# One core, 32 images of 32 channels: the sum r formed later, modes reordered earlier, a fuller end phase

## The chip, the cores and the metric

The kernel runs on one core of one Trainium2 chip. The metric is the device time of one execution in microseconds; the time before is the median of three executions.

## The reference

The input x has 32 images of 32 channels of 128 x 128 numbers, all in float32. Two layers are computed, each as x plus an operation on the group-normalised x (16 groups of 2 channels).

```python
# layer 0: a matrix square root of each channel by five Newton-Schulz steps
normA = jnp.sqrt(jnp.sum(A2 * A2, axis=(1, 2)))
Y = A2 / normA[:, None, None]; Z = I
for _ in range(5):
    T = 0.5 * (3.0 * I - jnp.matmul(Z, Y))
    Y = jnp.matmul(Y, T); Z = jnp.matmul(T, Z)
x = x + (Y * jnp.sqrt(normA)[:, None, None])
# layer 1: a spectral convolution; only 64 x 32 modes are kept
x_dht = jnp.fft.fftn(gn(x), axes=(2, 3)).real
top = jnp.einsum('bixy,ioxy->boxy', x_dht[:, :, :32, :32], weights1)
bot = jnp.einsum('bixy,ioxy->boxy', x_dht[:, :, -32:, :32], weights2)
x = x + jnp.fft.ifftn(out_dht, axes=(2, 3)).real   # out_dht holds top and bot, zeros elsewhere
```

## The kernel before

**Unit of work.** Layer 0 works on groups of four channels, 256 in all, each a tile of 128 x 512. `newton` (line 423) is a generator that carries one group: two calls of `quartic` (line 387), a few products between them, and a last sum into `xt`. A matrix product of a group is four matmuls of 128 x 128 (`products`, line 327), which in the profile are eight MATMUL records. `quartic` forms v from a product, turns it, adds `r` to make `w`, and multiplies v and w. `r` is the input plus a multiple of the identity: `plus_eye` (line 313), one GpSimd (POOL) instruction.

**Near and far groups.** For images 1 to 18 (`is_far`, line 339) the transpose of v goes partly through memory: VectorE (DVE) transposes blocks into `turn`, SyncE (SP) writes it to DRAM and reads it back as `w` (lines 394 to 409), and POOL adds r (line 411). For the other images TensorE (PE) transposes v, and DVE adds r from PSUM in the same instruction (line 415).

**Order of the work.** Nothing is left to a scheduler: the class `Engine` (line 75) keeps every engine's instructions in the order in which the program issues them. The main loop (line 1027) runs in rounds. In each round nine lanes take one step of their generator each; `yield from rest` (line 421) is two yields, so the next part of a group is issued two rounds later. A new group starts every three rounds (far) or five (near). Between lanes the loop steps other queues of generators: `norms` (scaling of the next group's input, `staged`, line 356), `posts` and `specs` (the forward transform of finished images, `forward` and `spectrum`), `prods` in two of three rounds (the products of modes with weights), and `backs` in one of three rounds, and when a batch is held (the inverse transform, `inverse`, line 863). When no lane is left, `tail` is true (line 1028) and all queues are stepped in every slot; the output stores then go out on ScalarE's (ACT's) queue instead of SP's (line 848).

**Where r stands before.** The first r of a group is issued at the end of `staged` (line 384), before the group starts, and waits there for ACT's scaling of `b`. The second is issued right after ACT's copy of `mb` (line 435). POOL takes its work in order, and other lanes' sums w stand behind these.

**Modes.** Images are taken in four sets of 20, 7, 3 and 2 (`GROUPS`). After the last image of a set its modes are multiplied: `wide_products` (line 603), `small_products` (line 659, sets of 7 and 3) and `last_products` (line 736, the last two images). The results go to DRAM (`od`) and come back per image: `load_products` (line 809) loads `or`; for the small sets a copy puts the modes in order as `ob` (line 872), 1.94 us on ACT in the median; then `inverse` issues 8 matmuls with `ob`, copies the result as `gt`, and runs two batches (e = 0, 1) of 8 matmuls, sums `yt` with DVE, unfolds them with POOL or DVE, and stores them. `load_input` (line 828) reads back the image into `yt` buffers, of which there are six, and three shared with `fold` at the end. `weights` (line 778) loads the last set's weights into tiles that the last lanes no longer need.

Of the kernel before, what the change touches and what calls it, by code (L numbers as in the profile page):

```python
# [36 lines left out]
P = 128  # L37
# [16 lines left out]
NB = 8  # L54
# [34 lines left out]
def conv_preact_kernel(  # L89
# [77 lines left out]

    def bank():
        return ps8.tile([P, 4, P], F32, tag="ps", name="ps")

    def root(v, n, tag):

# [183 lines left out]
    def staged(b, g, nm, sc, off, sn):  # L356

        m = four("x", has_more(b, g))
        xt, mb = raw.pop((b, g))

        def on_scalar(t, x, offset, scale, c):
            c = slice(c, c + 1)
            kept(
                nc.scalar.activation(t, x, AF.Identity, bias=offset[:, c], scale=scale[:, c])
            )

        for j in range(4):
            c = 4 * g + j
            if j < 2 or not is_far(b):
                kept(  # L370
                    nc.gpsimd.tensor_scalar(
                        m[:, j, :],
                        xt[:, j, :],
                        nm[:, c // 2 : c // 2 + 1],
                        sc[:, c : c + 1],
                        ALU.add,
                        ALU.mult,
                    )
                )
            else:  # L380
                on_scalar(m[:, j, :], xt[:, j, :], off, sc, c)
            on_scalar(mb[:, j, :], mb[:, j, :], off, sc, c)
            yield
        ready.append((xt, m, mb, plus_eye(mb, is_far(b), has_more(b, g))))
        yield

    def quartic(m, mb, r, far, more, wide):


        v = plus(m, -QA * MS, products(mb, m), "v", more)  # L390
        if far:


            t = four("turn", more)
            form = "p c (b i) -> p b c i" if wide else "p c (i b) -> p b c i"
            nc.vector.transpose(blocks(t), v.rearrange(form, b=4))
            held = dram.tile([P, 512], F32, name="turn", tag="turn", bufs=8)
            kept(nc.sync.dma_start(out=held, in_=t.rearrange("p c x -> p (c x)")))
            yield from rest
            w = four("w", more)  # L400
            wb = blocks(w).rearrange("p a c j -> p a (c j)")
            if wide:
                for b in range(4):
                    rows = slice(32 * b, 32 * b + 32)
                    src = held[:, P * b : P * b + P].rearrange("(a i) x -> i a x", a=4)
                    kept(nc.sync.dma_start(out=wb[rows], in_=src))
            else:
                src = held.rearrange("(a i) (b x) -> (i b) a x", a=4, b=4)
                kept(nc.sync.dma_start(out=wb, in_=src))
            yield from rest  # L410
            nc.gpsimd.tensor_tensor(w, w, r, ALU.add)
            w = blocks(w).rearrange("p a c j -> p c a j")
        else:
            yield from rest
            w = plus(transposed(v), 1.0, r, "w", more)
        yield from rest
        q = plus(products(v, w), QF / (16 * MS**4), eye, "q", more)
        yield from rest
        return q

    rest = (None, None)

    def newton(g, sn, xt, m, mb, r, far, more):


        q = yield from quartic(m, mb, r, far, more, False)
        my = four("my", more)
        y = my[:, :, 0, :]
        nc.scalar.mul(y, products(q, m), 1 / (MS * QF))
        yield from rest  # L430
        m = my[:, :, 1, :]
        nc.scalar.mul(m, products(q, y), MS / QF)
        yield from rest
        mb = taken(transposed(m), "mb", more)
        r = plus_eye(mb, far, more)
        yield from rest
        q = yield from quartic(m, mb, r, far, more, True)
        both = [bank().rearrange("p (j k) x -> p j k x", k=2) for _ in range(2)]
        for j in range(4):
            nc.tensor.matmul(both[j // 2][:, j % 2], q[:, j], my[:, j], start=True, stop=True)  # L440
        w, y = four("t", more), four("y4", more)
        for h in range(2):
            nc.scalar.mul(w[:, 2 * h : 2 * h + 2, :], both[h][:, :, 1, :], 1 / (MS * QF))
        for j in range(4):
            c = 4 * g + j
            nc.scalar.mul(y[:, j, :], both[j // 2][:, j % 2, 0, :], sn[:, c : c + 1])
        yield from rest
        t = plus(products(w, q), -0.5 * EYE / (1.5 * QF), eye, "t", more)
        yield from rest
        nc.vector.tensor_tensor(xt, products(t, y), xt, ALU.add)  # L450
        yield

    folds = {}
# [88 lines left out]
    def spectrum(b, u):  # L542
# [40 lines left out]
        if i == len(xs):  # L583

            for e, t in enumerate(diags):
                for l4 in range(4):
                    rows = slice(32 * l4, 32 * l4 + 32)
                    copy = nc.scalar.copy if l4 % 2 else nc.vector.tensor_copy
                    copy(
                        t.rearrange("p (m b l f) -> p m b l f", b=2, l=4, f=4)[rows, :, j, l4, :],  # L590
                        spec[rows, 8 * e : 8 * e + 8].rearrange("p k q (h f) -> p (k q h) f", f=4),
                    )
            yield
            return
        kept(
# [63 lines left out]
    def small_products(i):  # L659
# [40 lines left out]
        done = None  # L700
        for kk in range(KK):
            yield
            k2, e = divmod(kk, 2)
            wt, xk = wts[kk % len(wts)], xks[k2 % len(xks)]
            if not e:
                pm = bank()
            for t in range(8):
                for q in range(4):
                    nc.tensor.matmul(
                        pm[32 * q : 32 * q + 4 * n, 2 * e + t // 4, 32 * (t % 4) : 32 * (t % 4) + 32],  # L710
                        xk[:, :, 32 * e + 8 * q + t],
                        wt[:, t // 4, q, t % 4, :],
                        start=True,
                        stop=True,
                    )
            if kk + len(wts) < KK:
                load_weights(kk + len(wts))
            if done and not e:
                store(*done)
            if e:  # L720
                om = page(f"om{i}_{k2}")[:, 0:512]
                for j, rows in enumerate(parts):
                    copy = nc.vector.tensor_copy if j % 2 else nc.scalar.copy
                    copy(om[rows], pm.rearrange("p a x -> p (a x)")[rows])
                done = k2, om
                if k2 + len(xks) < KK // 2:
                    load_spectra(k2 + len(xks))
# [8 lines left out]
    def last_products(i):  # L736
# [4 lines left out]
        for kk in range(KK):  # L741
# [25 lines left out]
            if kk % 4 == 3:  # L767
                for f in range(4):
                    queue = nc.scalar if f % 2 else nc.sync
                    kept(  # L770
                        queue.dma_start(
                            out=od[i][f, kk - 3 : kk + 1].rearrange("k r x -> r k x"),
                            in_=om[f::4, :, f, :].rearrange("p (k h) o -> p k (h o)", h=2),
                        )
                    )
        yield

    def weights():
# [74 lines left out]
    def unfold():  # L853

        while sums:
# [4 lines left out]
                engine.tensor_tensor(yh, yh, d, op)  # L860
            stores.append((b, o, y))

    def inverse(b):


        more = where[b][1] < GROUPS[where[b][0]] - 1
        load_products(b)
        load_input(b, 0)
        yield
        ob = obs[b]  # L870
        if GROUPS[where[b][0]] <= NB:
            ob = inv.tile([P, 1024], F32, tag="ob", name=f"ob{b}", bufs=2)
            if where[b][0] == len(GROUPS) - 1:
                for h, copy in enumerate((nc.scalar.copy, nc.vector.tensor_copy)):
                    copy(
                        ob.rearrange("p (o h f l) -> p h o f l", h=2, f=4, l=4)[:, h],
                        obs[b].rearrange("p (f l h o) -> p h o f l", f=4, l=4, h=2)[:, h],
                    )
            else:
                nc.scalar.copy(  # L880
                    ob.rearrange("p (o t l) -> p o t l", t=8, l=4),
                    obs[b].rearrange("p (l t o) -> p o t l", l=4, t=8),
                )
        ob = ob.rearrange("p (e j m) -> p e j m", e=2, j=4)
        if more:
            load_products(b + 1)

# [8 lines left out]
        for e in range(2):  # L896
            gts.append(inv.tile([P, 4, P], F32, tag="gt", name=f"gt{b}_{e}", bufs=3))
            nc.scalar.copy(gts[e], pg[e])
        unfold()
        yield  # L900
        for e in range(2):
# [33 lines left out]
                load_input(b, 1)  # L935
            elif more:
                load_input(b + 1, 0)
            yield
        if not more:
            unfold()  # L940
# [194 lines left out]
```

## Time and profile before

| | |
|---|---|
| median of three executions | 3071.15 us (3064.79, 3072.52, 3071.15) |
| profiled execution | 3066.71 us |
| its span, first to last instruction | 3064.9 us |
| mean granted TensorE clock | 0.981 |
| PE, DVE, ACT, POOL busy | 95%, 73%, 54%, 65% |
| POOL sums r<-mb and r<-b | 256 each, mean 1275 ns |
| DMA | 636.41 MB, mean 208 GB/s |

In the profile's lines all recorded operations have line L83, since a helper issues them; so groups are told apart by the names of their tiles: `ps<-w,v` is a matmul into PSUM from w and v. A wait reads "engine tile <- engine tile that released it: us in total, times, longest". In a timeline a row is: start, duration, engine, line, operation, tiles, count, and in brackets the idle time before it with what ended it. PEld is TensorE's loading of weights, SPq and ACTq are issues of DMAs.

### The profile page before, as it was taken

What the parts mean: (1) busy time and instruction counts of PE and PEld (TensorE: products, weight loads), DVE (VectorE), ACT (ScalarE), POOL (GpSimd) and SP (SyncE); (2) the same over time, 40 slices, a digit from 0 to 9 for tenths busy, and PEclk for the clock granted to TensorE, in tenths of its full rate; (3) what the DMA queues carried; (4) which work ended last, traced back from release to release, by engine and by line L of the source; (5) the groups of instructions that cost most, each with busy time, mean ns of one, the idle gap of its engine ahead of it and who ended that gap; (6) DMA issues with size and microseconds to landing.
All of it is one profiled execution on the core that took longest, in us unless ns stands there. A gap on an engine that the chain in (4) does not pass through costs nothing. (4 is left out here: it accounts for less than half of the span.)

```text
span 3064.9 us, 73467 instructions
## 1 busy us (share of the span) xinstructions
PE 2897.2 (95%) x27076; PEld 2689.8 (88%) x27076; DVE 2244.1 (73%) x4255; ACT 1644.0 (54%) x4187; POOL 1997.2 (65%) x2312
## 2 busy tenths in 40 slices
PE   6999999999999999999999999999999998899984
PEld 6899999999989999989999888889889988888873
DVE  6778787868787788778876655777778766666564
ACT  3565555555656565656544445555555554554552
POOL 3667676767767677767764434778777764667453
PEclk9999999999999999999999999999999999999996
DMA  5476666667676767676742467767768677664675
GB/s 170 157 230 200 209 211 205 214 194 225 189 234 191 231 194 231 193 214 208 233 139 90 151 200 232 244 227 249 259 204 275 231 258 218 203 200 158 198 241 196
DMA packets 476660, 636.41 MB, mean 208 GB/s; under 512 B 97040, under 2 KB 257296, under 8 KB 476304
## 3 DMA queue, kind: packets, MB, share of 16 engines
q1 hardware_dynamic: 362976, 424.31, 43.2%
q10 hardware_dynamic: 113328, 207.41, 21.7%
q8 instruction: 217, 3.56, 0.5%
q14 instruction: 139, 1.14, 0.1%
HBM read 402.42 MB, written 229.11 MB: 206 GB/s over the span
## 5 line engine op out<-in xcount | busy, mean ns | idle before, releaser
L83 PE MATMUL ps<-my,q 128*128 128x128 f32 (+1 forms) x4096 | 734.5, 329 | 3.2 <-DVE w L83 1.5
L83 PEld LDWEIGHTS ps<-my,q 128*128 128x128 f32 x4096 | 625.6, 191 | 61.1 <-issue 6.8
L83 POOL TENSOR_TENSOR r<-mb,eye 128x512 f32<-128x512 f32 x256 | 326.5, 1275 | 431.6 <-ACT mb L83 413.3
L83 PE MATMUL ps<-w,v 128*128 128x128 f32 x4096 | 557.0, 279 | 34.3 <-POOL w L83 26.0
L83 PEld LDWEIGHTS ps<-w,v 128*128 128x128 f32 x4096 | 504.9, 193 | 53.9 <-POOL w L83 34.9
L83 ACT ACTIVATE b<-b,a_off,a_sc 128x128 f32<-128x128 f32 x1024 | 469.6, 493 | 150.9 <-issue 45.8
L83 DVE SCALAR_TENSOR_TENSOR q<-ps,eye 128x512 f32<-128x512 f32 x512 | 350.9, 685 | 225.5 <-PE ps L83 219.8
L83 ACT ACTIVATE my<-ps 128x512 f32<-128x512 f32 x512 | 306.4, 603 | 377.9 <-PE ps L83 361.7
L83 POOL TENSOR_TENSOR r<-b,eye 128x512 f32<-128x512 f32 x256 | 326.4, 1275 | 214.7 <-ACT b L83 160.4
L83 POOL TENSOR_TENSOR fold<-xt 128x256 f32<-128x256 f32 x512 | 363.6, 732 | 128.5 <-DVE xt L83 126.6
L83 POOL TENSOR_TENSOR w<-w,r 128x512 f32<-128x512 f32 x288 | 365.1, 1275 | 121.0 <-DMA w<-turn 94.8
L83 POOL TENSOR_TENSOR yt<-yt,d 128x512 f32<-128x512 f32 x248 | 310.8, 1279 | 147.7 <-ACT d L83 110.4
L83 ACT ACTIVATE t<-ps 128x256 f32<-128x256 f32 x512 | 191.4, 381 | 373.4 <-PE ps L83 361.5
L83 POOL TENSOR_SCALAR x<-xt,a_nm,a_sc 128x128 f32<-128x128 f32 x736 | 322.6, 451 | 18.6 <-DVE a_n L83 18.6
L83 ACT ACTIVATE y<-ps,a_t_s 128x128 f32<-128x128 f32 x1024 | 290.4, 374 | 0.0
L83 PE MATMUL ps<-y,t 128*128 128x128 f32 x2048 | 276.9, 279 | 8.1 <-DVE t L83 5.8
L83 PE MATMUL ps<-x,b 128*128 128x128 f32 x2048 | 277.3, 279 | 5.7 <-POOL x L83 5.7
L83 PE MATMUL ps<-x,q 128*128 128x128 f32 x2048 | 275.7, 278 | 3.2 <-DVE q L83 3.2
L83 PE MATMUL ps<-my,mb 128*128 128x128 f32 x2048 | 276.9, 279 | 0.0
L83 PE MATMUL ps<-q,t 128*128 128x128 f32 x2048 | 274.8, 277 | 0.5 <-DVE u L83 0.5
L83 DVE STREAM_TRANSPOSE turn<-v 128x512 f32<-128x512 f32 x288 | 264.8, 919 | 9.9
L83 PEld LDWEIGHTS ps<-y,t 128*128 128x128 f32 x2048 | 254.8, 194 | 13.0 <-issue 6.6
(121 smaller groups left out, 4464.7 us busy)
## 6 DMA issues: line engine op xcount, KB each, us to landing
turn<-turn SPq DMA_DIRECT2D x288, 256.0 KB
b<-in_x ACTq DMA_DIRECT2D x256, 256.0 KB
xt<-in_xt ACTq DMA_DIRECT2D x256, 256.0 KB
xs<-in_xs ACTq DMA_DIRECT2D x256, 256.0 KB
mid<-xt SPq DMA_DIRECT2D x256, 256.0 KB
yt<-mid SPq DMA_DIRECT2D x128, 512.0 KB
out<-yt SPq DMA_DIRECT2D x117, 512.0 KB
w<-turn SPq DMA_DIRECT2D x144, 256.0 KB
```

What stands on the lines that cost most here:

```text
L83: return self.tc.keep_in_program_order(issue(*args, **kw))
```

## The change

`plus_eye` is no longer called in `staged` and in `newton`; `quartic` calls it itself, two rounds after v for far groups (where the reload of `w` is issued) and one round after v for near groups, in place of one of its two plain yields. A new function `place` holds the copy that puts modes in order; `inverse` calls it for the next image of its set at the end of its last batch, with a step of its own for the first image of a set. In the end phase `inverse` loads both images' modes at its start and places the second image's modes right after the copies of `gt`. `small_products` yields twice at odd `kk`. A new function `warm` issues matmuls of 128 x 512 whose result nothing reads: two after the last group's `newton`, two after the last image's spectrum, nine after `last_products`.

```diff
+    def warm(n):
+        ps = bank()
+        for _ in range(n):
+            nc.tensor.matmul(ps, ident, tab[:, 0:512], start=True, stop=True)
...
-        ready.append((xt, m, mb, plus_eye(mb, is_far(b), has_more(b, g))))
+        ready.append((xt, m, mb))
...
             kept(nc.sync.dma_start(out=held, in_=t.rearrange("p c x -> p (c x)")))
             yield from rest
+            r = plus_eye(mb, far, more)
             w = four("w", more)
...
         else:
-            yield from rest
+            yield
+            r = plus_eye(mb, far, more)
+            yield
             w = plus(transposed(v), 1.0, r, "w", more)
...
         mb = taken(transposed(m), "mb", more)
-        r = plus_eye(mb, far, more)
         yield from rest
...
         nc.vector.tensor_tensor(xt, products(t, y), xt, ALU.add)
+        if not todo and lanes.count(None) == LANES - 1:
+            warm(2)
...
+            if tail:
+                warm(2)
             yield
             return
...
         for kk in range(KK):
             yield
+            if kk % 2:
+                yield
...
+        warm(9)
         yield
...
+    placed = {}
+
+    def place(b):
+        if GROUPS[where[b][0]] > NB:
+            placed[b] = obs[b]
+            return
+        ob = placed[b] = inv.tile([P, 1024], F32, tag="ob", name=f"ob{b}", bufs=2)
...
     def inverse(b):
...
         load_products(b)
+        if tail and more:
+            load_products(b + 1)
         load_input(b, 0)
         yield
-        ob = obs[b]
...
+        if b not in placed:
+            place(b)
+            if not tail:
+                yield
+        ob = placed.pop(b).rearrange("p (e j m) -> p e j m", e=2, j=4)
         if more:
             load_products(b + 1)
...
             nc.scalar.copy(gts[e], pg[e])
+        if tail and more:
+            place(b + 1)
         unfold()
         yield
...
             elif more:
                 load_input(b + 1, 0)
+                if b + 1 not in placed:
+                    place(b + 1)
             yield
```

More of the change, by code (lines that the diff above doesn't have):

```diff
@@ L383, in staged, with quartic @@
             yield
-        ready.append((xt, m, mb, plus_eye(mb, is_far(b), has_more(b, g))))
+        ready.append((xt, m, mb))
         yield
-    def quartic(m, mb, r, far, more, wide):
+    def quartic(m, mb, far, more, wide):
         v = plus(m, -QA * MS, products(mb, m), "v", more)
@@ L421, in conv_preact_kernel, with newton @@
     rest = (None, None)
-    def newton(g, sn, xt, m, mb, r, far, more):
-        q = yield from quartic(m, mb, r, far, more, False)
+    def newton(g, sn, xt, m, mb, far, more):
+        q = yield from quartic(m, mb, far, more, False)
         my = four("my", more)
@@ L434, in newton @@
         mb = taken(transposed(m), "mb", more)
-        r = plus_eye(mb, far, more)
         yield from rest
-        q = yield from quartic(m, mb, r, far, more, True)
+        q = yield from quartic(m, mb, far, more, True)
         both = [bank().rearrange("p (j k) x -> p j k x", k=2) for _ in range(2)]
@@ L861, in unfold @@
             stores.append((b, o, y))
+    placed = {}
[4 more added lines that the diff above has]
+        ob = placed[b] = inv.tile([P, 1024], F32, tag="ob", name=f"ob{b}", bufs=2)
+        if where[b][0] == len(GROUPS) - 1:
+            for h, copy in enumerate((nc.scalar.copy, nc.vector.tensor_copy)):
+                copy(
+                    ob.rearrange("p (o h f l) -> p h o f l", h=2, f=4, l=4)[:, h],
+                    obs[b].rearrange("p (f l h o) -> p h o f l", f=4, l=4, h=2)[:, h],
+                )
+        else:
+            nc.scalar.copy(
+                ob.rearrange("p (o t l) -> p o t l", t=8, l=4),
+                obs[b].rearrange("p (l t o) -> p o t l", l=4, t=8),
+            )
     def inverse(b):
@@ L867, in inverse @@
         load_products(b)
+        if tail and more:
+            load_products(b + 1)
         load_input(b, 0)
         yield
-        ob = obs[b]
[L871 to L884, printed above, removed]
+        if b not in placed:
[3 more added lines that the diff above has]
+        ob = placed.pop(b).rearrange("p (e j m) -> p e j m", e=2, j=4)
         if more:
```

## The prediction

> **What bounds the kernel now.** I read the page first, then all waits, the waits of TensorE by stretch, then timelines around its longest waits. The page's engine rows:
>
> ```profile
> PE 2897.2 (95%) x27076; PEld 2689.8 (88%) x27076; DVE 2244.1 (73%) x4255; ACT 1644.0 (54%) x4187; POOL 1997.2 (65%) x2312
> PEclk9999999999999999999999999999999999999996
> ```
>
> TensorE (PE) is the bound, in program order, at full clock except at the end. So a time can be saved only where PE stands still (3064.9 - 2897.2 = 168 us) or runs at half clock. The chain of waits names only the last 22 us, so the list of waits is the view to use:
>
> ```profile
> POOL r L83 <- ACT mb L83: 413.3, 124, 11.7
> POOL r L83 <- ACT b L83: 163.7, 73, 5.0
> PE ps L83 <- ACT ob L83: 37.6, 10, 11.2
> PE ps L83 <- POOL w L83: 26.0, 32, 2.2
> ```
>
> POOL loses 577 us waiting to form r, which by itself costs nothing, but PE loses 26.0 us to POOL's w, all between 100 and 1700 us, and 37.6 us to `ob`. How the first two are tied, in the timelines of POOL and PE:
>
> ```profile
> 501.50 1.27 POOL L83 TENSOR_TENSOR r<-mb,eye 128x512 f32<-128x512 f32 x1 [5.32 <-ACT mb L83]
> 502.74 1.28 POOL L83 TENSOR_TENSOR r<-b,eye 128x512 f32<-128x512 f32 x1
> 503.97 2.51 POOL L83 TENSOR_TENSOR w<-w,r 128x512 f32<-128x512 f32 x2
> 505.30 1.16 PE L83 MATMUL ps<-w,v 128*128 128x128 f32 x8 [1.31 <-POOL w L83]
> ```
>
> POOL stands 5.32 us before an r whose input ACT has not copied, does another r, and only then the w that PE waits for. I followed all 32 such PE waits back: in four (0.99, 2.25, 0.26 and 1.71, together 5.2 us) POOL waited for w's own reload; the other 20.8 us stand behind an r.
>
> The `ob` copy, from the timeline near 2577 us:
>
> ```profile
> 2577.12 1.95 ACT L83 COPY ob<-or 128x1024 f32<-128x1024 f32 x1
> 2579.13 2.08 PE L83 MATMUL ps<-tab,ob 64*128 64x128 f32 x16 [2.68 <-ACT ob L83]
> 2581.13 1.12 PE L83 MATMUL ps<-ident,v 128*128 128x128 f32 x4
> ```
>
> The copy is issued in the same step as its matmuls, so PE waits for nearly all of it; then it runs at half clock (2.08 us for 16 records that take 1.16 elsewhere). The waits by stretch give 8.2, 9.5 and 8.8 us in 2500-2700, 2700-2900 and 2900-3000: 26.5 us for images 20 to 29; the other 11.2 is image 30.
>
> The end, from the timeline of all engines:
>
> ```profile
> 3017.35 7.86 SPq L83 DMA_DIRECT2D od<-om  x8
> 3026.96 2.58 SPq L83 DMA_DIRECT2D or<-od  x4
> 3032.95 2.08 PE L83 MATMUL ps<-tab,ob 64*128 64x128 f32 x16 [11.18 <-ACT ob L83]
> 3046.09 2.08 PE L83 MATMUL ps<-tab,ob 64*128 64x128 f32 x16 [6.60 <-DVE ob L83]
> ```
>
> A round trip of modes through memory leaves all engines empty from 3024 to 3031.8, and image 31's modes are put in order only after image 30's work. From 3000 to 3015 and after 3025 most PE work is at half clock.
>
> **What the Trainium skill says.** "TensorE: Matmul & The Clock Gate", Part 1, puts the clock at half after an idle window of about 3.4 us, and at full after one busy window. The trace agrees in kind; a wait of 2.68 us was followed by half clock and one of 2.60 us (at 2682) was not, so the edge here lies lower. The same part says that ScalarE, VectorE and GpSimd are strict FIFOs: the POOL lines above show it. "DMA: Bandwidth & Descriptors", section on the anatomy of one DMA, says that a semaphore wait is held by the issuing sequencer before dispatch, so a load that waits for its buffer stops what is queued behind it. Before, the SP queue stood 3.1 us for one out<-yt that way.
>
> **The change, part by part.**
>
> *r two rounds behind.* The same 512 r sums at 1.27 us stay on POOL; for far images each comes two rounds (about 6 us: some 1027 rounds fill 3000 us, 2.9 us each) after its input, for near ones one round. Removed: up to 20.8 us of PE waits; lower bound 0, upper 34.9 (the weight loads' view of the same waits), all before 1700. ACT and DVE mostly stand waiting for PE (my<-ps 361.7, t<-ps 361.5), so few new waits should replace them: I take 90%, **-19 us**. The cost: b and mb are held two rounds longer. ACT's fetch needs a free b. With six buffers it takes that of the group three earlier, freed seven rounds before; with four (the last images) that of the group before, freed four rounds before. No cost, unless POOL falls four rounds behind (rival C).
>
> *Modes a step ahead.* The 1.95 us copy moves to the last step of the image before, five rounds earlier on ACT, where it hides beside PE's other work; queued behind it are ACT's evictions, whose slack is rounds. Its load is older still. Of 26.5 us I take 22, and 4 for the half clock that follows about half of these waits (1 to 2 us each). **-26 us**, bounds -13 and -35.
>
> *An extra yield at each odd kk of small_products.* In 2500-2560 PE waited 1.90, 3.77, 1.32 and 3.36 = 10.35 us for weights and spectra; a weight load is issued two kk ahead, which was three rounds and becomes four or five (16 kk in 36 rounds for 24). **-8 us** with the clock; bounds 0 and -14.
>
> *What that yield and the new first step shift.* Counting steps by the loop's rules: eight added yields at two prods steps per three rounds are 12 rounds, a group's first place is 3. The lanes still end in round 1027; image 29's mode matmuls go from round 1017 to the end phase, among last_products. That takes some 5.6 us of PE work (1.16 for the modes, four batches of 1.1) out of the stretch before 3000, **-5 us**, to the end phase.
>
> *The end.* POOL's unfolding of image 28 (2.5 us) now stands before the last fold: +1.5. PE warmer in 3000-3016: records at 2.05, 1.97, 1.98, 1.12 and 3.0 us would be 1.06, 1.09, 1.09, 0.60 and 1.76: at most -4.5, I take -4. A warm matmul is priced from 8 records of 128 columns in 0.89 us: two records of 512 columns, 0.89 us at full clock, 1.8 at half. warm(2) fits the 2.4 us gaps; warm(9), 8 us, fits the 11.2 us hole (at half clock 16 us, +5). A new wait: at last_products' start three pieces of image 28 are unstored and image 29 holds two of six yt buffers, so image 30's loads stand on SP until ACT has issued those stores, behind two copies of om, four od stores (0.76 each) and two gt copies (0.58), some 8 us, and landed (3). Behind them on SP: six od stores at 0.6 to 1, then image 29's second loads, then the last od and the or loads. In all I estimate the or loads 8 us later: +8; bounds 0 and +20. Image 31's modes beside image 30: PE's 6.60 goes, but DVE is busy 20 of the 23 us there, so -3. Sum of the end **+3 us**, bounds -9 and +20.
>
> Sum: -19 - 26 - 8 - 5 + 3 = -55. The profiled execution took 3066.7 (span 3064.9 and 1.8 around it), giving 3012; the median of the three times shown is 4.4 higher, so I predict **3016 us**.
>
> **Rivals.** About 0.3% (9 us) is what a measurement of this kernel can tell from no change.
>
> A, the forecast, 0.64: 3016, own range 2994 to 3036.
>
> B, the waits are passed on, 0.21: PE reaches the next instruction earlier and waits there for DVE or ACT (DVE v 8.4, DVE q 6.4, DVE w 9.8 already exist), and the end pays its upper cost. Half of the 58 us before the end, 29, and 8 more than now in the end: -21, about **3050**. For: PE's waits near 2669 are on DVE. Against: idle ACT.
>
> D, it hardly acts, 0.08: r was late only because PE was; w's reloads come as late as r did (POOL waits 94.8 us for them already), and the end eats the rest: **3068**.
>
> C, slower, 0.07: the longer-held b. If POOL's r falls behind its place by more than the four to seven rounds of slack (12 to 20 us), ACT stands at its fetch DMA with my, mb and t queued behind it, and PE follows. With 256 groups, 0.22 us per group cancels the 55 us; from 0.25 it is slower than before; 0.35 us gives 3016 + 90 = **3106**. For: POOL did fall 11.7 us behind at worst. Against: that was the wait for mb that now goes, and POOL is only 65% busy.
>
> **Range.** A and B hold 0.85; 2994 (A with the better bounds of r and ob) to 3058 (B with the end's bound) leaves out a bit over 0.15. Faster is A and B, 0.85; within 0.3% is D, 0.08; slower is C, 0.07.
>
> **What would show it.** POOL r<-mb waits near zero, PE waits on POOL w about 5 us, on ob none before 3000 us, plain<-in_wk waits under 3 us: each right. Wrong, if PE's waits on DVE v, q, w grow by as much; if ACT waits on fetches; if the or loads are issued as before, 13.7 us after the first of last_products' matmuls (my account of SP gives 22), or more than 34 us after it.

## The result, and the profile after

The changed kernel takes **3047.6 us** (median of four, 3046.1 to 3053.3), the kernel before, beside it, 3071.8; the ratio is 0.9931 with a 95% interval of 0.9916 to 0.9946. It is faster by about 24 us; 55 were forecast. The time lies in the range, 32 us above the predicted 3016. The profiled execution took 3046.5 us, its span is 3044.4.

The engine rows of its page:

```profile
PE 2894.3 (95%) x27102; PEld 2682.8 (88%) x27102; DVE 2273.0 (75%) x4261; ACT 1644.0 (54%) x4187; POOL 1987.4 (65%) x2306
...
PEclk9999999999999999999999999999999999999996
```

PE is still the bound, and it stands still for 150 us instead of 168. Six rows from the list of all waits, in order of size:

```profile
POOL r L83 <- ACT mb L83: 79.6, 26, 9.2
...
DVE w L83 <- POOL r L83: 56.3, 31, 5.9
...
PE ps L83 <- DVE v L83: 21.1, 12, 9.8
...
PE ps L83 <- DVE w L83: 19.6, 16, 4.0
...
PE ps L83 <- ACT ob L83: 7.6, 1, 7.6
...
PE ps L83 <- POOL w L83: 4.2, 4, 1.7
```

Lines 1, 5 and 6 show what was wanted: POOL stands before an r on `mb` for 79.6 us instead of 413.3 (the forecast had it near zero), PE's waits for w from POOL fell from 26.0 to 4.2, those for `ob` from 37.6 to one of 7.6, in the end. Lines 2 to 4 are new or have grown. DVE waits 56.3 us for POOL's r, and in the kernel before 0.9; PE waits 21.1 for DVE's v (8.4 before) and 19.6 for DVE's w (9.8).

The end, from the timeline of SP and then that of PE:

```profile
2960.94 28.45 SPq L83 DMA_DIRECT2D yt<-mid  x4
2989.49 9.24 SPq L83 DMA_DIRECT2D od<-om  x6
...
3005.56 6.96 SPq L83 DMA_DIRECT2D or<-od  x4
```

```profile
2964.24 1.97 PE L83 MATMUL ps<-fold,tab 128*32 128x504 f32 x12 [14.37 <-POOL fold L83]
...
2997.37 9.90 PE L83 MATMUL ps<-tab,ident 128*128 128x512 f32 x18 [11.18 <-ACT om L83]
...
3015.98 2.08 PE L83 MATMUL ps<-tab,ob 64*128 64x128 f32 x16 [7.63 <-ACT ob L83]
```

Image 30's loads hold SP for 28.45 us, and what is queued behind them, SP's stores of modes, starts at 2989. From the waits of SP in this stretch, what it stands for:

```profile
SPq L83 <- DMA out<-yt: 37.0, 5, 26.0
```

These are the stores of image 28, whose buffers the loads need. Some 15 us of the hold lie before last_products' first matmul (2975.81), when no mode is ready to be stored; it ends 13.6 us after that matmul, where the forecast had 8 and 3. The or loads follow 29.8 us after it; before it was 13.7, and the forecast gave 22.

To see where time is won, the last sum `xt` of each group was read in the timeline of DVE. In the profiled executions the sum of group 128 comes 30.4 us earlier than before, that of group 208 22.9, the last one (the lanes' end) 40.6: at 2959.7 instead of 3000.3. But from there to the end of the span it takes **84.7 us instead of 64.6**. The forecast had -58 for the lanes and +3 for the end; measured are -40.6 and +20.1.

This split hides one thing. From the timelines of PE and DVE before that sum:

```profile
2946.99 1.16 PE L83 MATMUL ps<-y,t 128*128 128x128 f32 x8 [0.79 <-DVE t L83]
2947.99 1.88 PE L83 MATMUL ps<-tab,ident 128*128 128x512 f32 x4
...
2958.49 1.29 DVE L83 TENSOR_TENSOR yt<-ps,yt 128x512 f32<-128x512 f32 x2 [11.55 <-DMA yt<-mid]
2959.70 0.68 DVE L83 TENSOR_TENSOR xt<-ps,xt 128x512 f32<-128x512 f32 x1
```

PE has finished the lanes' last product at 2948.2. In DVE's order a sum `yt` of the inverse transform now stands in front of the last `xt`, and its loads have not landed, so DVE waits 11.55 us and PE, after two of the warm matmuls, 14.37 for `fold`. In the kernel before PE ends that product at 3000.2 and `xt` follows at once. Told by PE, the lanes came 52.1 us earlier, near the forecast's 58, and what follows takes 96.2 us instead of 64.7. All kernels of the table below with the copies a step ahead show such a gap, of 7 to 13 us; the four others (r_only, r_near2, slow_only, slow_late30) show none.

### The profile page after: what moved, and what is told of

It reads as the page before. It is cut to its first block, busy times and chain, and to the rows that moved or that the text cites. A ratio compares the mean times of both kernels' runs of the same rounds, so it can differ in the third digit from the quotient of the medians.

```text
span 3044.4 us, 73265 instructions
## 1 busy us (share of the span) xinstructions
PE 2894.3 (95%) x27102; PEld 2682.8 (88%) x27102; DVE 2273.0 (75%) x4261; ACT 1644.0 (54%) x4187; POOL 1987.4 (65%) x2306
## 5 line engine op out<-in xcount | busy, mean ns | idle before, releaser
L83 POOL TENSOR_TENSOR w<-w,r 128x512 f32<-128x512 f32 x288 | 366.7, 1274 | 372.6 <-DMA w<-turn 320.2
L83 PE MATMUL ps<-w,v 128*128 128x128 f32 x4096 | 553.0, 278 | 22.9 <-DVE w L83 12.1
L83 POOL TENSOR_TENSOR yt<-yt,d 128x512 f32<-128x512 f32 x242 | 304.4, 1282 | 277.9 <-ACT d L83 245.3
L83 POOL TENSOR_TENSOR r<-mb,eye 128x512 f32<-128x512 f32 x256 | 326.5, 1275 | 79.7 <-ACT mb L83 79.6
L83 PEld LDWEIGHTS ps<-x,b 128*128 128x128 f32 x2048 | 252.6, 194 | 11.0 <-POOL x L83 6.0
```

Of the source, the lines that this page charges most:

```text
L83: return self.tc.keep_in_program_order(issue(*args, **kw))
```

## The experiments

Each edit is to the kernel named with it, and each kernel was timed in five rounds. "Advance" is how much earlier than in the kernel before the sum of group 128 and the lanes' end come, "end" is from there to the end of the span, all in the one profiled execution. One execution speaks for the advance within some 10 us only: an edit that acts after 2400 us (`slow_only`) shows -8.2 at group 128. The kernel before, timed anew beside each of them, took 3066.8 to 3073.7 us. So the ratios decide, and the advance tells where.

| kernel | median us | ratio (95%) | advance 128 | lanes' end | end |
|---|---|---|---|---|---|
| changed kernel | 3047.6 | 0.9931 (0.9916 to 0.9946) | 30.4 | 40.6 | 84.7 |
| r_only | 3055.6 | 0.9958 (0.9942 to 0.9973) | 29.8 | 15.4 | 65.3 |
| r_near2 | 3031.3 | 0.9882 (0.9866 to 0.9897) | 29.9 | 40.0 | 65.5 |
| nearr | 3033.3 | 0.9879 (0.9860 to 0.9898) | 18.8 | 43.4 | 82.2 |
| place_only | 3048.7 | 0.9932 (0.9911 to 0.9954) | -0.4 | 21.1 | 66.5 |
| place_nophase | 3033.8 | 0.9880 (0.9862 to 0.9899) | -0.7 | 37.4 | 68.2 |
| after_nophase | 3038.0 | 0.9900 (0.9879 to 0.9920) | 29.4 | 47.6 | 82.1 |
| slow_only | 3068.1 | 0.9989 (0.9979 to 0.9999) | -8.2 | 15.9 | 81.5 |
| slow_late30 | 3066.9 | 0.9997 (0.9987 to 1.0007) | 0.0 | 20.2 | 85.3 |
| noslow | 3029.7 | 0.9871 (0.9850 to 0.9892) | 27.0 | 38.9 | 66.4 |
| late30 | 3035.2 | 0.9884 (0.9866 to 0.9901) | 33.5 | 49.6 | 79.0 |
| late30_no9 | 3036.5 | 0.9900 (0.9884 to 0.9916) | 33.3 | 43.6 | 79.5 |
| nowarm | 3047.4 | 0.9919 (0.9899 to 0.9938) | 29.1 | 38.3 | 81.8 |
| best | 3026.7 | 0.9860 (0.9836 to 0.9884) | 28.4 | 42.1 | 66.0 |
| best_nophase | 2997.4 | 0.9776 (0.9758 to 0.9794) | 33.4 | 76.0 | 65.7 |
| place_only_ts | 3037.3 | 0.9887 (0.9864 to 0.9910) | -2.8 | 32.3 | 66.9 |
| place_nophase_ts | 3033.5 | 0.9871 (0.9853 to 0.9889) | -3.2 | 38.8 | 66.6 |
| after_ts | 3047.9 | 0.9917 (0.9896 to 0.9937) | 25.0 | 38.2 | 82.0 |
| best_nophase_ts | 3002.3 | 0.9772 (0.9751 to 0.9794) | 20.6 | 57.4 | 65.7 |

### The end: is it SP's hold, or image 29's work?

`late30` is the changed kernel with image 30's loads at the end of last_products instead of its start:

```diff
-        for e in range(2):
-            load_input(B - GROUPS[i], e)
         for kk in range(KK):
...
+        for e in range(2):
+            load_input(B - GROUPS[i], e)
         warm(9)
```

> The changed kernel with one thing moved: image 30's four input loads are issued at the end of last_products instead of at its start, so that nothing stands before the od stores on SP's queue. Theory S (SP held 28 us by these loads delays the od stores, and through their pages the rest of the end): the time from the last newton's xt sum to the end falls from 84.7 us to 66-72, and the whole from 3047.6 to 3030-3037. Rival I (image 29's own work fills the end, the held queue is beside it): the end stays at 80 us or more, the whole at 3042-3050.

`noslow` is the changed kernel without the extra yield:

```diff
             yield
-            if kk % 2:
-                yield
             k2, e = divmod(kk, 2)
```

> The changed kernel without the extra yield in small_products; image 29 is then done with the lanes, three rounds later than in the kernel before. Theory S: image 30's loads find free buffers, the end takes 60-66 us; the lanes end 5 to 15 us later than in the changed kernel, since the weights are waited for again (10 us) and image 29's work is back: 3032-3044 in all. Rival Y (the yield is most of what was gained before the end): the lanes end 25 us later or more, 3050-3060 in all.

`slow_only` is the kernel before with that yield alone, `slow_late30` the same with image 30's loads late.

> The kernel before with the extra yield of small_products alone. Theory S (it pushes image 29's last batches into the end, where image 30's loads then hold SP's queue, and gives 8 to 15 us before): the end 10 to 18 us longer, 3070-3080 in all, slower than the kernel before or equal. Rival Y (as my forecast had it, 8 + 5 us gained, 3 lost): 3058-3063.

> The kernel before with the extra yield of small_products and image 30's input loads at the end of last_products. Theory S (the yield alone gains 16 us before the end and gives 17 back in it, where SP is held by those loads): the end falls from 81.5 to 68-75 us, 3054-3062 in all. Rival I (image 29's work itself fills the end): 3065-3070.

With the hold gone the end is 79.0 us, not the 66 to 72 of a hold that costs it all; without the yield it is 66.4. The yield alone, without any of the other parts, makes it 81.5, and 85.3 without the hold. The five kernels that have both the hold and the parts of the changed kernel (it, nearr, nowarm, after_nophase, after_ts) have ends of 81.8 to 84.7, the two without the hold (late30, late30_no9) 79.0 and 79.5. So the hold is worth some 2 to 6 us of this end, and in the pair with the yield alone nothing. The rest comes with the yield. What it moves past the lanes' end is image 29's inverse transform; that this work is what lengthens the end is read from the traces, since no run moves it alone. How the end begins without the yield, in the SP timeline of noslow:

```profile
2979.94 11.33 SPq L83 DMA_DIRECT2D od<-om  x8
2993.03 2.58 SPq L83 DMA_DIRECT2D or<-od  x4
```

SP's eight od stores go out together and the or loads take 2.58 us to issue. In slow_late30, with no hold either, from the timeline of all engines:

```profile
3019.80 5.23 SPq L83 DMA_DIRECT2D or<-od  x4
...
3033.46 2.08 PE L83 MATMUL ps<-tab,ob 64*128 64x128 f32 x16 [24.01 <-ACT ob L83]
```

Here the or loads come beside other loads and stores, and PE waits 24.01 us for the modes. Busy time in the end says the same: DVE 28.9 us before, 31.0 in noslow, 37.4 in slow_late30, 39.3 in the changed kernel; ACT 15.3, 15.4, 20.5, 20.8; POOL 13.1, 14.7, 17.2, 20.2. Before the lanes' end this work lay beside PE; here it stands among copies `om` and sums that PE and each other wait for.

noslow came out better than either theory had it, slow_only near the theory that lets the end grow, and slow_late30 where the rival had it: without the hold nothing is gained.

late30 is 12 us faster than the changed kernel, and in the profiled executions only 6 of that are in the end; its lanes' end is 9 us earlier, although the edit comes after it. That 9 stays unexplained beyond the spread of executions.

The yield also pays little on the lanes once r and the modes are early: the lanes end at 2961.3 without it and at 2959.7 with it. Told by PE's last product it is some 5 us (52.1 us ahead beside 46.4 in noslow, and 54.7 in nearr beside 49.9 in best), within the spread of executions, and DVE then waits longer for the last sum (11.5 us beside 7.5). Its shift sets other work side by side. In the changed kernel, on SP and then on DVE:

```profile
2785.78 10.18 SPq L83 DMA_DIRECT2D diag<-xs  x16
```

```profile
2807.73 1.29 DVE L83 TENSOR_TENSOR yt<-ps,yt 128x512 f32<-128x512 f32 x2 [11.65 <-DMA yt<-mid]
```

The loads of an inverse batch come behind 16 loads of spectra, and DVE, with v queued behind its `yt`, stands 11.65 us, and PE behind it 9.76. The other such wait is the one of 11.55 us before the last `xt`. Between 2440 and 2960 DVE's waits for yt<-mid sum to 23.9 us; in noslow to 2.1 in all.

### The sum r: far groups and near groups

`r_only` is the kernel before with the move of r alone. `r_near2` is r_only, and `nearr` the changed kernel, with the r of near groups issued in v's own step:

```diff
         else:
-            yield
             r = plus_eye(mb, far, more)
-            yield
+            yield from rest
             w = plus(transposed(v), 1.0, r, "w", more)
```

> The kernel before with the move of r alone. Theory N (worth 25 to 30 us in the far stretch, of which near groups give back about 15 as DVE waits for POOL's r): group 128's xt sum 25 to 33 us earlier than before, the lanes' end 10 to 20 us earlier, 3050-3060 in all. Rival Q (my forecast's step: 19 us in the far stretch, nothing lost after): 3050-3054 with the advance kept from group 160 to 255.

> The changed kernel with r of near groups issued in the step of v, two rounds before w uses it instead of one. Theory N (DVE's w waits for POOL's r, 56 us in all, and passes some of it to PE, which ate 15 us of the gain between 1700 and 2450 us): DVE w <- POOL r falls below 15 us, the lanes end 8 to 15 us earlier, 3033-3040 in all. Rival P (these waits are DVE's idle time beside a busy PE): no change over 4 us, 3043-3050.

> The kernel before with the move of r alone, and the near groups' r in the step of v, two rounds before its use instead of one. Theory N (one round is too near: DVE's w waits for POOL's r and PE for w): 3040-3046 against 3055.6 of the move with one round. Rival O (the move alone lost only 4 us between groups 128 and 208, so DVE's wait is mostly idle time): 3051-3057.

For the far groups the move gives more than its forecast: the thirteen kernels of the table with it stand 19 to 34 us ahead at group 128, ten of them 27 or more, and the six without it -8 to 0. Up to that sum PE stands still for 40.5 us in r_only instead of 60.6, and is busy for 1324.4 instead of 1334.1: two thirds of the gain are the waits that went; why the same matmuls also take less is open. For the near groups it costs. From all waits, r_only first, then r_near2:

```profile
DVE w L83 <- POOL r L83: 48.6, 25, 5.6
...
PE ps L83 <- DVE w L83: 18.2, 12, 3.4
```

```profile
PE ps L83 <- DVE w L83: 9.7, 5, 3.9
...
DVE w L83 <- POOL r L83: 8.1, 6, 3.9
```

One round after v is too late: DVE, in order, stands for r, and PE behind it for w. One round earlier both are back near their old size, and the kernel is some 23 us faster (ratios 0.9958 and 0.9882, intervals apart). r_only's lead of 29.8 at group 128 melts to 15.4 at the lanes' end, r_near2's grows to 40.0. In the changed kernel the same edit gains 14 us. The one-round wait's price was as expected for r_only and nearr; r_near2 gained more than its 3040 to 3046.

### Modes a step ahead, and the extra first step

`place_only` is the kernel before with `place` and the pair of modes at the end. The large first set has no copy, but its first image also gets the extra step; `place_nophase` and `after_nophase` leave it out of place_only and the changed kernel:

```diff
-            if not tail:
+            if not tail and GROUPS[where[b][0]] <= NB:
                 yield
```

> The kernel before with place alone, the second image's early placing at the end included, and no warm matmuls, no yield, r as before. Theory F (my forecast's step holds: 26 us before the end and 3 in it): 3040-3046. Rival G (PE takes over only part of the waits): 3050-3058. Image 29 stays out of the end, so neither expects the end to be longer than 64 us.

> The kernel before with place alone, without the extra step ahead of the first set's first image, which has no copy to bring forward. Theory M (the step, not the copy, costs what place fell short of): no loss by group 208 (within 3 us of the kernel before, against -9.5), the lanes' end 30 to 40 us earlier than before, 3030-3040 in all. Rival K (the step costs only beside the mended r): 3045-3050, as with it.

> The changed kernel without that one extra step, all else kept: r one round ahead for near groups, the yield, the warm matmuls. Theory M: the advance at group 208 stays above 27 us against 22.9, the lanes' end 10 to 25 us earlier, the end still 80-86 us, 3024-3038 in all. Rival K: 3044-3049.

The copy alone is worth 37 us at the lanes' end, more than its 26; the step takes 15 us back, and 10 in the changed kernel. place_only fell between its two expectations, since it holds a gain and a loss; place_nophase and after_nophase came in as the theory of a costly step had it, the latter at the edge. Between groups 128 and 192 place_only and place_nophase stand within 1 us of each other, and part then, 9 us by group 208. What happens near there, in the timeline of all engines of place_only:

```profile
2259.78 4.92 POOL L83 TENSOR_TENSOR yt<-yt,d 128x512 f32<-128x512 f32 x4
2260.46 5.63 DVE L83 TENSOR_TENSOR b_inv<-b_r 128x1 f32<-128x1 f32 x1
2264.68 1.39 POOL L83 TENSOR_TENSOR fold<-xt 128x256 f32<-128x256 f32 x2
2266.01 0.67 DVE L83 SCALAR_TENSOR_TENSOR v<-my,ps 128x512 f32<-128x512 f32 x1
...
2266.74 1.65 PE L83 MATMUL ps<-my,q 128*128 128x256 f32 x3 [5.09 <-DVE v L83]
```

A product of 128 x 1 lasts 5.63 us while POOL sums four yt and a fold; v, behind it, is late, and PE stands 5.09 us. The Trainium skill, "SBUF — State Buffer", section "Summary: rules for kernel authors", says that a DVE instruction with two SBUF inputs and a GpSimd one that reads SBUF block each other fully, the later one until the first is done. The trace agrees that the later one is held, but it does not go on after one POOL instruction: a sum yt takes 1.23 us here (four in 4.92), and DVE's product ends at 2266.09, with the last of six POOL instructions in a row. The step of the first set moves the inverse transform by one, and more such sums of yt meet such products: those instructions of DVE (TENSOR_TENSOR with no PSUM input) last 142.8 us together in place_only, 128.1 in place_nophase.

To try this, the last four kernels issue b_inv as a TENSOR_SCALAR with the second factor as its scalar:

```diff
-        nc.vector.tensor_mul(r, s[:, 1:2], s[:, 2:3])
+        nc.vector.tensor_scalar(r, s[:, 1:2], s[:, 2:3], 1.0, ALU.mult, ALU.mult)
```

> place_only with the sum of the group norm's last factor, b_inv<-b_r of 128x1, issued as a TENSOR_SCALAR with a scalar from memory (which b_r<-b_v,b_r shows at 272 to 275 ns in all 32 cases) instead of a TENSOR_TENSOR (158 to 5631 ns, 28.3 us in all, 23 more than 32 times the shortest). Theory M, the extra step costs through VectorE's instructions that GpSimd holds up: the 23 us go, PE gets most of it where VectorE is late, 3048.7 falls to 3028 to 3039. Rival E, the stretched instruction is only a symptom of a VectorE that has slack, and the loss sits elsewhere: 3045 to 3052.

> The same edit in the kernel without the extra step, where b_inv takes 18.8 us in all, 14 more than at its shortest. M: 3033.8 falls by at most 14, to 3020 to 3032, and the distance between this pair, 15 us before the edit, shrinks to 8 or less. E: 3030 to 3037, and the distance stays 12 to 18.

> The same edit in the changed kernel, b_inv 23.5 us in all, 18.4 more than at its shortest. M: 3047.6 falls to 3030 to 3041. E: 3044 to 3051.

> The same edit in the fastest kernel so far (no extra step for the first set, r of near groups in v's step, no extra yield), b_inv 18.5 us in all, one of them 6.1 us. M: 2997.4 falls to 2983 to 2994. E: 2994 to 3001.

The row of that instruction in the answer for its tile (duration in ns: shortest, median, longest), in place_only and in place_only_ts:

```profile
L83 DVE TENSOR_TENSOR b_inv<-b_r x32: 158/500/5631, 172.8 to 2989.4; 128x1 f32<-128x1 f32 x32
```

```profile
L83 DVE TENSOR_SCALAR b_inv<-b_r x32: 212/214/215, 170.3 to 2978.1; 128x1 f32<-128x1 f32 x32
```

The stretch of this instruction is gone. place_only gains 11 us by it and place_nophase nothing that can be told, so the distance of the pair falls from 15 to 4: there the stretched products are most of the step's price. But the changed kernel and best_nophase gain nothing from the same edit (0.9917 beside 0.9931, 0.9772 beside 0.9776), against the theory. In after_ts the hold is in part still there, one instruction further on:

```profile
L83 DVE SCALAR_TENSOR_TENSOR spec<-b_v,b_inv,spec x32: 165/206/5395, 181.0 to 2976.1; 32x1 f32<-32x1 f32 x32
```

Three of these products last 3.31, 5.39 and 4.99 us; before the edit three of them lasted 3.25, 3.85 and 4.99. In place_only_ts none lasts over 1.19. So what the step costs in the changed kernel, 10 us, and in best, 26 by the ratios, is measured, and its path there stays open. In best the TENSOR_TENSORs with no PSUM input last 166.7 us, in best_nophase 136.1, as if it were the same path; the edit was not tried on best.

### Warm matmuls, and the best version

`nowarm` is the changed kernel without all three `warm` calls, `late30_no9` is late30 without `warm(9)`; nothing reads their results. `best` is the changed kernel with the edits of noslow and nearr; `best_nophase` also has the step left out of the first set.

> The changed kernel without the 13 warm matmuls. Theory S: the nine stand 9.9 us in front of image 29's last batch on PE, while the path runs over the od stores and loads; without them that batch comes earlier and the copies for ob are free sooner: 0 to 6 us faster, 3041-3048. Rival W (they keep PE's clock up for the end): 3 to 6 us slower, 3050-3054.

> The changed kernel with image 30's loads at the end of last_products and without the nine warm matmuls (the other four stay). Theory H (once SP is no longer held, the nine warm matmuls of 8 us in front of image 29's last batch are what comes last: its sums, pages and the copies of ob stand behind them): the end falls from 79.0 to 71-74 us, 3027-3031 in all. Rival (SP's stores are still last, or the warm clock is worth as much): 3033-3038, as with them.

> The changed kernel without the yield in small_products and with the near groups' r in the step of v. Theories N and S together add up (14 and 18 us against the changed kernel): 3012-3020, the lanes' end 12 us earlier than in the changed kernel, the end 62-67 us. Rival: both act on the same idle time: 3026-3032.

> The kernel without the yield in small_products and with the near groups' r in the step of v, further without the extra step ahead of the first image of the first set, whose modes need no copy: its inverse transforms are back in the rounds of the kernel before. Theory M (those three rounds put the inverse steps against the lanes so that DVE and PE wait, some 9 us by group 208): the advance at group 208 rises by 6 to 10 us, 3017-3022 in all. Rival R (that loss is chance or belongs to r): 3024-3030.

The warm matmuls have no effect that can be measured, alone or once the hold is gone: after `warm(9)` and the batch of 1.15 us behind it PE waits 7.63 us for `ob`, and the next matmuls are at half clock again (2.08 us). The first pair, at 2947.99, was meant for a gap of 2.46 us before `fold`; the gap is now 14.37, and the matmuls after it take the 1.97 us of before. Both runs had this outcome among their expectations. best gains over noslow less than nearr does over the changed kernel (0.9860 beside 0.9871, intervals overlap): the edits overlap, as its rival had it. best_nophase, expected near 3020, beats both kernels by far: 2997.4 us, 69 less than the 3066.8 of the kernel before beside it:

```profile
PE 2881.1 (96%) x27102; PEld 2675.0 (89%) x27102; DVE 2252.9 (75%) x4257; ACT 1642.0 (55%) x4187; POOL 1995.7 (67%) x2310
```

It does the matmuls of the changed kernel in a span 54 us shorter; PE stands for 109 us. It keeps the r of far groups, the copies of modes a step ahead and the warm matmuls, and drops the three steps that cost.

## Why the prediction went wrong, step by step

**r two rounds behind, -19: right in kind, too small, and one half of it wrong.** PE's waits went as told (26.0 to 4.2; the text gave about 5); POOL's for `mb` fell to 79.6, not to near zero. For the far groups it is worth some 28: the waits that went (21.8 us), and less busy time of PE. The step that failed is "No cost": it asked only whether b and mb are held too long. For near groups r moves to one round after v with w one round behind it, and DVE's w waits on it. In the list of waits of the kernel before it was 0.9 us, so no row showed it; the place of r among POOL's other work had to be counted. Price: some 23 us in r_only, 14 in the changed kernel.

**Modes a step ahead, -26: right and too small (37), but the extra first step was never costed for the set that has no copy.** The text counted that step's rounds for image 29 alone. For the first set it buys nothing and costs 15, 10 or 26 us, as the other parts stand. Nor was it seen that a `yt` sum comes to stand before the lanes' last sum, for 7 to 13 us. A moved phase was costed at nothing since only rounds were counted, not which instructions then meet.

**The extra yield, -8 and -5 for the shift: about right alone for the lanes (-15.9, and -20.2 in slow_late30), wrong in company.** PE's waits for weights went (plain<-in_wk from 6.6 us to 0.2 in slow_only; the changed kernel's list has none), those for spectra only changed (3.8 us for xs<-in_xs before, 4.9 for diag<-xs now), and DVE's waits for yt<-mid were added, and the lanes' last sum comes hardly sooner than without it (2959.7, 2961.3). Its cost, in the end, stays.

**The end, +3: the step that failed most.** Measured is +20.1, at its upper bound, and +31.5 counted from PE's last product of the lanes. The hold of SP was seen and sized at 8 us of delay (the or loads came 16 us later); without it the end is 2 to 6 us shorter. The larger miss came with the yield, and by the traces it is image 29: the text moved "5.6 us of PE work" to the end and took it to cost nothing there, as if PE bounded the end. It also carries 8 us of DVE's work and 5 of ACT's, and a batch's loads and stores, into a chain of copies, DMAs and waits: 13 to 21 us (66.4 to 79.0 from noslow to late30, 64.6 to 85.3 in slow_late30). The clock's -4 did not come (nowarm). And a wait's length alone does not tell what the clock does: in the kernel before, full clock still followed a wait of 2.91 us (at 2918.51), and half clock one of 2.25 (at 626.84).

**The parts' sum.** By the ratios r_only, place_only and slow_only save 0.42%, 0.68% and 0.11%, 1.21% or 37 us; all together save 0.69%, 21 us. r, place and warm without the yield save 1.29%, 40 us: these two add up. The loss in company is the yield's, 18 us.

**The rivals.** The time is that of B, 3050, which had half of the 58 lost and the end at 8 worse. Its mechanism is there (PE's waits for DVE v, q, w grew from 24.6 to 49.6 us), but 41 of 58 came through (52 by PE), and the end took the rest; that B's number was met is in part luck, since it had more lost before the end and less in it. C, ACT held at its fetch by b, did not decide: POOL is early now (it waits 320.2 us for w<-turn, 94.8 before), and PE's waits for ACT's my only went from 0.3 to 1.8 us. D is refuted by r_near2 and place_nophase.

## What to carry to other kernels

Work moved out of a stretch that one engine bounds has to be priced anew where it lands: the yield that moved 5.6 us of PE's work, with what goes with it, cost 13 to 21 us in an end that is a chain of round trips. The last instruction of a stretch can stand behind something else in its engine's order, so the cut between two stretches is best read on more than one engine. When an instruction moves earlier or later, count its distance to each reader in steps, for each kind of group by itself; and a step added to a shared loop shifts every user of the loop, those too that have nothing to gain. Try the parts alone and left out: three small steps here hid two thirds of the gain that the others gave (0.69% of 2.24% was left).

## What the hardware showed that was not expected

- A DVE TENSOR_TENSOR of 128 x 1, 0.158 us at its shortest, lasted up to 6.82 us (best, 2233.47) while POOL ran sums over SBUF back to back. As TENSOR_SCALAR, with the same two factors, it took 0.212 to 0.215 us in all 32 cases. The form alone is no safeguard: another TENSOR_SCALAR, a_v<-a_vg of 128 x 32, lasted 5.30 us in after_ts (2401.55) while POOL summed.
- Warm matmuls of 128 x 512 took 9.90 us for 18 records after a wait of 11.18, and 7.99 in late30 without such a wait, the 8 priced at full clock; two before the last modes (4 records) 3.62 us, the price at half clock. Neither moved the time.
- The same four or loads were issued in 2.58 us in noslow, and in 5.23 and 6.96 us where loads and stores of an image lay beside them.
